# A cross-attention kernel with layer norm: a new hand-written order for its first twelve and last eight pairs of row tiles, one residual product taken from TensorE, the statistics of tile 62 computed on ScalarE, the last store in two halves

## The chip, the cores and the metric

The kernel runs on one core of one Trainium2 chip. The metric is device microseconds (us) of that core, the median of several runs. Engines are named as in the profile: PE is TensorE's matrix products, PEld its weight loads, DVE is VectorE, ACT is ScalarE, POOL is GpSimd, SP is SyncE, which here only issues DMA transfers. Transfers can also be issued by ACT and POOL, and then take time on those engines' own instruction streams.

## What is computed

`x` has 4 batches of 2048 rows of 512 numbers, `ctx` has 4 batches of 77 rows; there are 16 heads of 32 columns. Everything is float32.

```python
q = x @ wq;  k = ctx @ wk;  v = ctx @ wv                   # then split into 16 heads of 32
s = q @ k.T / sqrt(32);  s = where(mask, -inf, s)          # 77 keys per row and head
out = softmax(s) @ v @ wo + x                              # residual
y = (out - mean(out)) / sqrt(var(out) + 1e-5) * gamma + beta
```

## The kernel before, in words

The 8192 rows are 64 tiles of 128 rows. Two tiles make a pair (numbers 0 to 31); four tiles make a group, for which the queries are computed together. A float32 matrix product with 512-wide weights is made of three products of rounded parts (high by high, high by low, low by high), so each projection of one tile's worth of output is 12 matrix instructions.

Nothing of the order is left to a scheduler. The string `ORDER` lists the whole program as some 2,100 words. A letter says what, a number says for which tile, pair or group part, and a part number follows a dot. The program emits the words in that order, so each engine executes its own words strictly in the order in which they stand; between engines only data and buffers make anything wait. The words that matter here, with the lines of the kernel before:

- On PE: `Qn` (line 290) a query product of 12 instructions; `Sn` (L414) the scores of tile n, 64 small instructions into four PSUM banks; `Vn` (L507) weights by values for pair n, 32 instructions into two banks, and `Wn` (L522) the same for one tile alone, used for tiles 62 and 63; `On` (L579) the output projection of tile n, 12 instructions; `Xn` (L566) adds the residual `x` into tile n's PSUM bank by a product with an identity matrix, ahead of `On`.
- On DVE: `Tn.j` (L431) masks four heads' scores and takes their row maxima (4 instructions, each followed by the reading of an accumulator); `qn` (L304) copies queries out of PSUM; `rn` (L456) reciprocals of the softmax sums; `tn` (L482) transposes a tile's weights in 32x32 blocks; `bn.i` (L540) and `dn` make the low part of the attention output; `+n` (L588) adds the residual and frees the bank; `$n` (L591) adds it in place in PSUM; `sn` (L630, L632) mean and variance of a tile; `yn` (L649) subtracts the mean and multiplies by gamma, in place; `zn` (L652) scales by the inverse deviation and adds beta.
- On ACT: `en.j` (L446) four heads' exponentials with their sums; `an.i` and `cn` (L536) the high part of the attention output; `in` (L269) casts of `x`; `kn` (L617) and `%n` (L645) scale and shift a tile by its statistics.
- On POOL: `nn` (L461) multiplies the exponentials by the reciprocals, `mn.i` (L473) half of that; `jn` (L273) low parts of `x`; `fn` (L621, L622) multiplies by gamma and adds beta; `un` (L636, L637) and `@n` (also L641) the inverse deviation of a tile.
- Transfers: `Pn.c` with a last letter s, a or g (L493, issued by SP, ACT or POOL): one of 12 copies that move pair n's transposed weights into the layout that `Vn` reads; `Un.c` the same for one tile, ahead of `Wn`; `xn` loads rows, `gn` loads transposed rows, `wn` (L625) stores a finished tile.

So a tile goes through PE scores, DVE maxima, ACT exponentials, DVE reciprocals, POOL normalisation, DVE transposition, 12 transfers, PE weights-by-values, ACT and DVE splitting, PE output projection, residual, statistics and the final pass. A tile's final pass has two forms: `@`, `%`, `f` put it on ACT and POOL, and `u`, `y`, `z` put it on DVE. The string `SLOTS` gives every buffer of every pool by hand: its row "mm" says which of the 8 PSUM banks each product takes, so a product can only start when the bank's last reader, some word on DVE or ACT, is done. The string `PADS` gives for each `Q` and `O` a number of empty instructions on PE's sequencer between its 12 matrix instructions.

From about pair 6 to pair 22 the order repeats every two tiles. Before that stand the weight preparation, keys and values; after it there are no more queries to load and the tiles drain.

Of the kernel before, what the change touches and what calls it, by code (L numbers as in the profile page):

```python
# [33 lines left out]
for b in range(4):  # L34
# [17 lines left out]
e1.3 F2 T2.2 j5 t0 e1.1 Q6 i4 F1 g7 r1 Y1 e2.0 F3 L1 T3.2 n1 Q5 x1 T3.1 e2.1 Y0 q6 R2 T3.3 e3.3 j4 t1 B0 e2.3 P0.6s  # L52
x3 e3.1 B2 D0 i7 q7 Z0.s T3.0 P0.10s e3.0 q5 P0.2s S4 P0.7s D2 e3.2 Z3.s S6 T4.0 P0.4s e2.2 G1 B1 g6 G2 Z1.s G0
Z2.s T4.3 e4.3 P0.3s r3 G3 P0.0s Q9 n3 T4.1 P0.1s T4.2 e4.2 P0.9s D1 P0.8s r2 n2 e4.0 t3 P0.5s Q8 P0.11s e4.1 T6.0
T6.3 i6 t2 Q10 e6.0 r4 P1.0s T6.2 n4 P1.8s T6.1 e6.1 S5 P1.2s q10 x2 q8 Q11 e6.2 j6 P1.11s T5.3 P1.1s T5.2 e5.3
P1.10s T5.1 P1.9s t4 j7 e6.3 P1.4s S7 P1.6s Q14 T7.0 P1.7s e7.0 q9 P1.3s r6 T7.3 P1.5s n6 e7.3 T7.2 x0 q11 Q13 g8
e7.2 T5.0 Z13.s T7.1 g9 e7.1 Z6.s M16.4 Z10.s S9 q13 Z11.s e5.0 q14 V0 r7 t6 n7 e5.1 V1 a0.1 T9.1 e5.2 t7 Q15 a1.0
b0.1 a1.1 P3.4s r5 T9.2 Z12.s n5 e9.2 b1.0 P3.1s b1.1 P3.8s O2 e9.1 T9.3 P3.2s t5 P3.0s a0.0 P3.5s i8 T9.0 P2.2s S8
e9.0 +2 j8 P3.3s T8.3 O3 P2.6s e9.3 b0.0 P3.6s T8.1 P3.10s T8.2 i9 P2.8s r9 s2 P3.11s S10 e8.2 j9 P3.9s +3 O1 P3.7s
T8.0 e8.0 P2.9s q15 s3 P2.3s n9 e8.1 P2.7s T10.0 P2.4s O0 T10.1 e8.3 x7 T10.2 v1 P2.1s +1 g11 e10.0 T10.3 P2.11s  # L60
Q12 +0 Z9.s k3 r8 Z4.s s1 n8 e10.3 P2.5s t9 Z5.s k2 g10 S11 s0 e10.1 f3 P2.0s V3 t8 e10.2 Q19 T11.1 P4.3s f2 a3.1
q12 P2.10s a3.0 e11.1 T11.3 w3 b3.0 x5 T11.0 Z8.s i11 v0 q19 P4.0s e11.0 b3.1 O7 x6 r10 P4.6s T11.2 n10 k1 P4.2s
S12 P4.4s k0 +7 P4.10s S13 e11.3 T12.1 f1 w2 s7 Q16 P4.9s e11.2 T12.3 P4.5s T12.2 P4.1s e12.2 T12.0 f0 P4.8s t10 x4
# [747 lines left out]
```

## Time and profile before

| what | us |
|---|---|
| median of 3 runs | 512.98 (512.11 to 513.15) |
| the profiled execution | 511.94 |
| its span, first to last instruction | 510.1 |
| PE busy | 499.4 |
| DVE busy | 470.7 |
| ACT busy | 463.2 |
| POOL busy | 421.6 |

The span is the time from the first to the last record of the profiled execution; the 1.8 us between it and the time of the same execution lie outside the records. Busy time is the time in which an engine has at least one instruction in work. "Waits" tell for each engine what released it after an idle time. A "timeline" lists single instructions with start and duration; matrix instructions overlap, so the time that one takes from the next is the distance of two starts, not the duration shown.

### The profile page before, as it was taken

Reading aid. Unit: us, or ns where it says so; the run is one execution under the profiler, and the core shown is the slowest. Engines: PE = TensorE matmul, PEld = TensorE weight load, DVE = VectorE, ACT = ScalarE, POOL = GpSimd, SP = SyncE. Lnnn points to the kernel's source line nnn. Section 1 sums busy time; section 2 is a strip of 40 time slices with the busy share of each in tenths; the row PEclk is TensorE's granted clock in tenths of the full one; section 3 lists DMA queues with packets and bytes.
Section 4 is the critical chain, followed back from the end, with each engine's and each line's share of the span. In section 5 each row is a group of like instructions: output and inputs, shape, how many; then the busy total and the mean of one; then the engine's idle time right before and its main releaser. Section 6 shows DMA issues by size and latency. Waiting matters only on the chain.

```text
span 510.1 us, 21817 instructions
## 1 busy us (share of the span) xinstructions
PE 499.4 (98%) x6835; PEld 384.7 (75%) x6835; DVE 470.7 (92%) x2565; ACT 463.2 (91%) x2221; POOL 421.6 (83%) x389
## 2 busy tenths in 40 slices
PE   8999999999999999999999999999999999999994
PEld 6987777777777777777777877777777767776673
DVE  5798999999999999999999999999999899999897
ACT  5699999998999999999999999999999999899620
POOL 2573756999978898989889898888899689999896
PEclk9999999999999999999999999999999999999999
DMA  8947767867977687687778678685787895688655
GB/s 304 399 137 216 191 171 173 251 190 239 267 222 219 189 238 209 200 243 207 229 206 245 200 217 238 187 243 161 218 223 210 225 224 168 174 242 259 176 174 214
DMA packets 58995, 110.95 MB, mean 217 GB/s; under 512 B 9398, under 2 KB 11790, under 8 KB 58886
## 3 DMA queue, kind: packets, MB, share of 16 engines
q1 hardware_dynamic: 55094, 102.22, 68.5%
q0 software_dynamic: 2512, 5.84, 4.1%
q10 hardware_dynamic: 1280, 1.51, 1.1%
q8 instruction: 60, 0.98, 0.9%
q14 instruction: 49, 0.40, 0.3%
HBM read 41.79 MB, written 16.78 MB: 115 GB/s over the span
## 4 chain that ended last, share of the span: by engine, by line
PE 79%; POOL 6%; DVE 5%; DMA 4%; ACT 2%; issue 1%; SPq 1%; DVEq 0%; POOLq 0%
PE pq L290 32%; PE po L579 25%; PE sc L414 10%; PE pa L507 9%; DMA PT<-B 3%; ACT pbuf L446 2%; DVE B L482 2%; PE pv L341 2%; POOL PT L493 1%; PE pk L313 1%; DMA stage_a<-wk 1%; DVE pbuf L431 1%; POOL o L621 1%; POOL mvt L637 1%; POOL o L622 1%
## 5 line engine op out<-in xcount | busy, mean ns | idle before, releaser
L446 ACT ACTIVATE pbuf<-pbuf,nm 128x77 f32<-128x77 f32 x1024 | 352.5, 351 | 4.2 <-DVE nm L431 4.0
L446 ACT ACTIVATION_READ_ACCUMULATOR pbuf<-pbuf,nm 128x1 f32 x1024 | 196.2, 192 | 0.0
L431 DVE CUSTOM_DVE_ANT_0 pbuf<-sc,mb 128x77 f32<-128x77 f32 x1024 | 171.3, 233 | 8.0 <-PE sc L414 4.3
L461 POOL TENSOR_TENSOR pbuf<-pbuf,ri 128x1232 f32<-128x1232 f32 x63 | 142.8, 2267 | 30.4 <-DVE ri L456 26.2
L579 PE MATMUL po<-woh,AH 128*128 128x512 f32 x256 | 102.2, 399 | 1.8 <-DVE nm L431 1.4
L290 PE MATMUL pq<-xth,wqh 128*128 128x512 f32 (+1 forms) x256 | 101.3, 396 | 0.3
L579 PE MATMUL po<-woh,AL 128*128 128x512 f32 x256 | 100.0, 391 | 0.2
L579 PE MATMUL po<-wol,AH 128*128 128x512 f32 x256 | 99.8, 390 | 0.0
L482 DVE STREAM_TRANSPOSE B<-pbuf 128x1280 f32<-128x1280 f32 x64 | 95.9, 1500 | 2.9 <-POOL pbuf L473 1.4
L290 PE MATMUL pq<-xtl,wqh 128*128 128x512 f32 (+1 forms) x256 | 98.1, 383 | 0.0
L290 PE MATMUL pq<-xth,wql 128*128 128x512 f32 (+1 forms) x256 | 98.1, 383 | 0.0
L431 DVE DVE_READ_ACCUMULATOR2_ANT nm<- 128x1 f32 x1024 | 84.7, 83 | 0.0
L273 POOL TENSOR_TENSOR xtl<-xtf,xth 128x1024 fp32r<-128x1024 f32 x28 | 67.2, 2406 | 5.8 <-ACT xth L269 5.8
L622 POOL TENSOR_TENSOR o<-o,bet 128x512 f32<-128x512 f32 x52 | 67.2, 1293 | 4.1
L414 PEld LDWEIGHTS sc<-kct,q 32*64 32x64 f32 x4096 | 51.3, 130 | 22.8 <-issue 10.8
L621 POOL TENSOR_TENSOR o<-o,gam 128x512 f32<-128x512 f32 x52 | 68.3, 1314 | 0.2 <-issue 0.2
L414 PE MATMUL sc<-kct,q 32*64 32x77 f32 x4096 | 60.7, 238 | 0.0
L507 PE MATMUL pa<-PT,vsb 96*32 96x256 f32 x992 | 59.7, 382 | 0.0
L579 PEld LDWEIGHTS po<-woh,AH 128*128 128x128 f32 x256 | 48.0, 188 | 14.8 <-PE pa L507 1.0
L290 PEld LDWEIGHTS pq<-xth,wqh 128*128 128x128 f32 x256 | 48.0, 188 | 12.4 <-issue 1.2
L579 PEld LDWEIGHTS po<-woh,AL 128*128 128x128 f32 x256 | 48.0, 188 | 11.5 <-DVE AL L540 1.4
L579 PEld LDWEIGHTS po<-wol,AH 128*128 128x128 f32 x256 | 48.1, 188 | 9.9 <-issue 0.5
(120 smaller groups left out, 640.0 us busy)
## 6 DMA issues: line engine op xcount, KB each, us to landing
PT<-B SPq DMA_DIRECT2D x339, 128.0 KB
xtf<-xT SPq DMA_DIRECT2D x28, 512.0 KB
o<-x SPq DMA_DIRECT2D x56, 256.0 KB
out<-o SPq DMA_DIRECT2D x56, 256.0 KB
PT<-B POOLq DMA_DIRECT2D x26, 128.0 KB, 4.2
stage_a<-wk SPq DMA_DIRECT2D x4, 256.0 KB
stage_b<-wo SPq DMA_DIRECT2D x4, 256.0 KB
stage_a<-xT SPq DMA_DIRECT2D x2, 512.0 KB
```

Source lines behind the costliest of these rows:

```text
L273: nc.gpsimd.tensor_tensor(l[:, c : c + 2], fx.pop((g, c)), xh[g][:, c : c + 2].bitcast(F32), ALU.subtract)
L290: nc.tensor.matmul(pq, w[:, c, m * P : (m + 1) * P], r[g][:, c, rs], start=(n == 0), stop=(n == 11))
L341: nc.tensor.matmul(pv[: rows.stop - rows.start], ctx_s[c][i][:, rows], v[c], start=(n == 0), stop=(n == 11))
L414: mm = nc.tensor.matmul(sc[j][r0 : r0 + SR, g * NK : (g + 1) * NK], qs[q, g, rs.start + r0 : rs.start + r0 + SR], kct[q, g, t // TPB, keys ...
L431: nc.vector.tensor_tensor_reduce(pb[:, h // 2, (h % 2) * NK : (h % 2 + 1) * NK], scs[t][j][:, g * NK : (g + 1) * NK], mb[:, t % TPB, keys_ ...
L446: nc.scalar.activation(pb[:, h // 2, (h % 2) * NK : (h % 2 + 1) * NK], pb[:, h // 2, (h % 2) * NK : (h % 2 + 1) * NK], AF.Exp, bias=nmax[t ...
L461: nc.gpsimd.tensor_tensor(pv, pv, rv.to_broadcast((P, NP, 2, NK)), ALU.mult)
L482: nc.vector.transpose(bt.rearrange("p c q r -> p q c r"), pbuf[t % NPB].rearrange("p q (c r) -> p q c r", c=5),)
L507: nc.tensor.matmul(pas[b, g // 2][HD * j : HD * (j + 1), (g % 2) * BLK : (g % 2 + 1) * BLK], vsb[:, 2 * b // TPB, h % 2, HD * (h // 2) : H ...
L579: nc.tensor.matmul(pos[t], a[:, c, rs], w[:, c, :], start=(first and c == 0 and n == 0), stop=(c == NC_D - 1 and n == 2),)
L621: nc.gpsimd.tensor_tensor(o, o, gam, ALU.mult)
L622: nc.gpsimd.tensor_tensor(o, o, bet, ALU.add)
```

## The change

The order of the words is new in two stretches. From pair 0 to about pair 9 and from tile 52 to the end the same words stand in another order, and "mm", the other buffer rows and `PADS` follow. Between them the order of the words on PE, DVE and ACT is as before, except for a few loads of `x` that stand a few words earlier or later. The empty instructions of `PADS` are 1,719 in place of 1,468.

These words differ:

- `X49` is gone; tile 49's residual is added by `$49` on DVE.
- Tile 48's final pass is `u48`, `y48`, `z48` in place of `@48`, `%48`, `f48`.
- `$52` and `$58` become `+52` and `+58`.
- `s62` becomes `=62`, new: two passes of ACT over tile 62's PSUM bank, the first a copy scaled by -1/512 whose accumulator gives minus the mean, the second a square of value minus mean whose accumulator gives 512 times the variance. `u62` and `y62` take those instead.
- `z63` and `w63` become `>63.0 <63.0 >63.1 <63.1`, new: the final pass and the store of tile 63 in halves of 256 columns, the first half stored by SP, the second by ACT.
- Of the transfers, `P25.4`, `P27.0` and `P29.6` go from SP to POOL, `P26.9` from ACT to SP, `U62.8` from SP to ACT, `U63.3` from POOL to ACT.

The order of the words on PE in the last stretch, before and after:

```text
before: S52 V23 S53 Q59 Q58 Q57 S54 Q56 V24 S55 O46 X49 O49 S56 O47 S57 V25 O48 Q61 Q63 S58 Q62 V26 S59 Q60 O50
        S60 O53 X51 S61 O51 V27 S62 O52 V28 O55 S63 O57 O56 X63 V29 X62 O54 O58 V30 O59 O61 O60 W62 W63 O62 O63
after:  S52 V23 S53 Q58 Q56 Q57 S54 Q59 S55 O46 V24 S56 O47 O49 V25 S57 O48 Q61 S58 Q62 Q63 Q60 S59 V26 O50
        S60 X51 O53 S61 O51 S62 V27 O52 V28 O55 O54 S63 X62 O57 X63 V29 O56 O58 V30 O59 O61 O60 W62 W63 O62 O63
```

The ends of `ORDER`, and the code:

```diff
-a30.0 U62.9s U63.10g s58 U62.11a U62.7s U63.7g O59 %53 $57 U62.1s U63.6g a30.1 U63.3g s57 U62.6s U62.10a @58 w52
-b30.0 U63.1a U63.2s b30.1 u57 O61 U63.8a y57 f53 U63.5a s54 U62.0a z57 %58 y54 w57 U63.9a O60 $59 f55 +61 s61 s59
-W62 @61 $60 w55 w53 s60 W63 u54 c62 w50 %61 u59 d62 O62 c63 u60 y59 z59 f61 d63 w59 z54 w56 y60 O63 z60 f58 w61 s62
-w49 w54 y62 w60 s63 u62 w58 y63 u63 z62 z63 w62 w63
+s57 m63.0 P30.7a %55 b29.1 O58 u57 t62 %53 f55 %52 t63 U62.10a U62.2s V30 U62.4a U62.1s U62.8a +58 U63.0s f53 a30.0
+s58 U63.4s O59 U62.0a $56 a30.1 U63.11s b30.0 U62.3a U62.9s s54 U62.11a U62.7s U63.7g U63.1a y57 U63.6g U62.6s
+U63.9a s56 U62.5g U63.8a U63.10g b30.1 O61 U63.2s u56 $59 U63.5a w55 z57 U63.3a @58 O60 y56 w46 f52 %58 +61 s61 s59
+W62 @61 y59 W63 $60 c62 u59 y54 f58 c63 d62 O62 %61 z59 s60 w59 w57 d63 u60 w53 y60 O63 w52 u54 =62 z60 w58 f61 y62
+w60 z54 z56 w54 s63 u62 w61 y63 w56 u63 z62 w62 >63.0 <63.0 >63.1 <63.1
...
+    def stats_act(t):
+        mv = mvs[t, 1] = tiny.tile([P, 4], F32, tag="mvt", bufs=64 - LATE, name=f"mvt_{t}")
+        nc.scalar.activation(od[t], pos[t], AF.Copy, scale=-1.0 / D, accum_out=mv[:, 3:4])
+        nc.scalar.activation(od[t], pos[t], AF.Square, bias=mv[:, 3:4], accum_out=mv[:, 1:2])
+        by_act.add(t)
+
     def rsqrt_one(t):
         mv = mvs[t, 1]
-        nc.gpsimd.tensor_tensor(mv[:, 2:3], mv[:, 1:2], eps[:, :1], ALU.add)
+        if t in by_act:
+            nc.gpsimd.tensor_scalar(mv[:, 2:3], mv[:, 1:2], 1.0 / D, EPS, ALU.mult, ALU.add)
+        else:
+            nc.gpsimd.tensor_tensor(mv[:, 2:3], mv[:, 1:2], eps[:, :1], ALU.add)
         nc.gpsimd.tensor_tensor(mv[:, 2:3], mv[:, 2:3], mhalf[:, :1], ALU.pow)
...
     def centre(t):
         o = pos.get(t, od[t])
-        nc.vector.scalar_tensor_tensor(o, o, mvs[t, 1][:, 0:1], gam, ALU.subtract, ALU.mult)
+        m, op = (3, ALU.add) if t in by_act else (0, ALU.subtract)
+        nc.vector.scalar_tensor_tensor(o, o, mvs[t, 1][:, m : m + 1], gam, op, ALU.mult)
...
+    def finish_half(t, i):
+        cols = slice(i * D // 2, (i + 1) * D // 2)
+        nc.vector.scalar_tensor_tensor(
+            od[t][:, cols], pos[t][:, cols], mvs[t, 1][:, 2:3], bet[:, cols], ALU.mult, ALU.add
+        )
+
+    def store_half(t, i):
+        cols = slice(i * D // 2, (i + 1) * D // 2)
+        (nc.sync, nc.scalar)[i].dma_start(out[t * P : (t + 1) * P, cols], od[t][:, cols])
```

More of the change, by code (lines that the diff above doesn't have):

```diff
@@ new lines @@
+b26.1 e59.1 z48 x53 X51 f42 T60.1 w49 O53 P28.8s T60.0 k47 T60.3 e59.3 T60.2 t58 P28.4g e60.0 S61 P28.10g x55
+P28.2g e60.2 r59 P28.3s O51 T61.3 P28.6g n59 P28.1s +53 e60.1 P28.5s T61.0 w48 T61.2 x56 T61.1 e60.3 S62 f47 P28.0s
+t59 V27 e61.1 r60 T62.1 a27.0 T62.0 n60 P29.9s O52 a27.1 s51 e61.3 P29.11s T62.3 x52 b27.0 w42 e61.2 s53 P29.1g x60
+V28 P29.0g P29.8s $50 k46 P29.7g P29.2s T62.2 P29.6g e61.0 b27.1 P29.4g x54 O55 t60 P29.3g P29.10s a28.0 u51 x59
+a28.1 @53 e62.3 r61 +52 n61 b28.1 O54 e62.1 b28.0 y51 +55 P29.5a f46 t61 e62.2 S63 z51 e62.0 X62 T63.2 w51 O57
```

129 lines of the change are left out of this document (62 added, 67 removed).

## The prediction

> **What bounds the kernel now.** I read the busy time by stretches first, then the chain of waits in order of time, then the waits of the last stretch, then single instructions.
>
> ```profile
> 68.00:85.00 17.00, 17.00 (x303) 12.71 (x303) 16.59 (x82) 16.47 (x81) 9.53 (x5) 1.00 0.61 158
> ...
> 289.00:306.00 17.00, 17.00 (x220) 13.32 (x219) 16.38 (x83) 16.66 (x82) 15.48 (x14) 1.00 0.71 208
> ```
>
> The columns are the stretch, its length and the busy time (with instructions) of PE, PEld, DVE, ACT, POOL, then the granted clock. PE is busy in all of 17.00 us, early and in the middle. DVE, at 16.38, and ACT, at 16.66, have 0.6 and 0.3 us to spare. So what PE is spared in these stretches comes off the end, and what the others are spared does not.
>
> ```profile
> 440.00:460.00 20.00, 20.00 (x372) 14.20 (x370) 19.79 (x127) 20.00 (x109) 18.79 (x18) 1.00 0.71 201
> 460.00:478.00 18.00, 17.14 (x183) 11.96 (x180) 17.86 (x87) 18.00 (x100) 16.15 (x24) 1.00 0.89 248
> 478.00:495.30 17.30, 16.91 (x94) 12.21 (x94) 15.67 (x30) 5.27 (x10) 15.81 (x22) 1.00 0.55 157
> ```
>
> Here it is different. From 440 to 478 PE, DVE (19.79 of 20.00, 17.86 of 18.00) and ACT are all full, and PE already stands still for 0.86 us in the second row. After 478 the exponentials are over and ACT has room.
>
> ```profile
> PE po L579 <- DVE nm L431: 1.4, 2, 0.9
> ...
> DVE B L482 <- POOL pbuf L473: 1.4, 1, 1.4
> ...
> DVE pbuf L431 <- PE sc L414: 0.8, 1, 0.8
> DVE B L482 <- POOL pbuf L461: 0.8, 2, 0.5
> ...
> DVE o L588 <- PE po L579: 0.7, 1, 0.7
> ...
> DVE po L591 <- PE po L579: 0.4, 1, 0.4
> PE po L579 <- DVE xth L652: 0.4, 1, 0.4
> ```
>
> These are the waits from 395 us, where the two orders part, to 510 us: sum, times, longest. DVE stands idle for 1.4 + 0.8 + 0.8 + 0.7 + 0.4 = 4.1 us in all, and PE's products wait for DVE for 1.4 + 0.4 us. So PE and DVE hold each other up in turn. The last 115 us are bound by these two together, and the question of this change is how much of DVE's 4.1 us of idleness the new order fills.
>
> **The change part by part.**
>
> *PE's own work.* The price of a product, and of a change of kind, from the chain of waits (start, length, what):
>
> ```profile
> 109.40 0.88 PE sc L414 x55
> 110.28 5.68 PE po L579 x24
> 115.96 2.72 PE pq L290 x12
> 118.68 0.88 PE sc L414 x55
> ...
> 148.42 5.66 PE pq L290 x24
> 154.08 5.44 PE po L579 x24
> 159.52 0.88 PE sc L414 x53
> 160.40 1.86 PE pa L507 x32
> ...
> 468.10 2.89 DVE B L482 x2
> ```
>
> A product that follows a product takes 2.72 us. A run of three takes 118.68 - 110.28 = 8.40, a run of four 159.52 - 148.42 = 11.10: 0.24 and 0.22 more than three and four times 2.72. So each run of products costs some 0.22 once, whatever its length. Counting the words, before `S20` the runs fall from 17 to 15, between there and `S52` they stay 16, and behind `S52` they fall from 16 to 15. The early part is worth -0.44 us, the late one -0.22. The empty instructions cost nothing that I can see: `PADS` gives the stretch at 110 0 to 8 per product and the one at 148 12 to 22, and the runs cost the same in both. More than 22 does not occur in the new `PADS`.
>
> ```profile
> 416.90 1.02 PE L566 MATMUL po<-o,ident 128*128 128x512 f32 x2
> 417.36 0.80 PE L579 MATMUL po<-woh,AH 128*128 128x512 f32 x1
> ...
> 420.96 0.95 PE L414 MATMUL sc<-kct,q 32*64 32x77 f32 x64
> ```
>
> `X49` with `O49` takes 420.96 - 416.90 = 4.06, which is 1.34 over a product. About 0.3 of it is a wait inside for the low part of pair 24, so the residual product itself is worth 1.0. Behind `S52` PE thus has 1.2 us less to do (1.6 if the wait goes too).
>
> *DVE's own work.* Starts of its instructions in a full stretch, and of maxima:
>
> ```profile
> 397.46 0.23 DVE L431 CUSTOM_DVE_ANT_0 pbuf<-sc,mb 128x77 f32<-128x77 f32 x1
> 397.61 0.23 DVE L431 CUSTOM_DVE_ANT_0 pbuf<-sc,mb 128x77 f32<-128x77 f32 x1
> ...
> 485.34 0.69 DVE L591 TENSOR_TENSOR po<-po,xth 128x512 f32<-128x512 f32 x1
> 485.94 0.74 DVE L652 SCALAR_TENSOR_TENSOR xth<-po,mvt,bet 128x512 f32<-128x512 f32 x1
> 486.59 0.69 DVE L630 BATCH_NORM_STATS2 st<-po 128x6 f32<-128x512 f32 x1
> ...
> 487.42 0.67 DVE L591 TENSOR_TENSOR po<-po,xth 128x512 f32<-128x512 f32 x1
> ```
>
> By starts, `$` costs 0.60, `z` 0.65 and `s` 0.83 (`y`, of the same kind as `z`, 0.65); a maximum costs 0.15. The change adds `$49`, `y48`, `z48` and removes `s62`: 0.60 + 0.65 + 0.65 - 0.83 = +1.1. `z63` in halves is two instructions, an estimate of +0.2. DVE has 1.3 us more to do. ACT loses `%48` and one transfer issue, POOL loses `f48`; ahead of the last exponentials neither is what PE waits for, so I give nothing for them.
>
> *DVE's idleness.* Adding up each engine's own words from `S52` on, waits left out, shows who is late. Ahead of `O61` PE has 12 `S` (0.88), 8 `V` (1.86), 4 `X` (1.0), 22 products and 15 runs: 92.6 us. Up to the low part of pair 30, which `O61` needs, DVE has 48 `T` (0.65), 14 transpositions (1.44), 13 `s`, 12 residuals, 8 `y` and `z`, 16 `b` and 8 `q` (0.60, as `$`), 14 reciprocals and two mask rows (0.3): 92.1. So DVE could be there first, and idles. In the new order PE has 91.4 and DVE, with `$49`, one `s` and one `y` more, 94.2: DVE has little reason to idle any more, and PE waits for it. For pair 24 and `O49` the same count gives 21.5 on DVE against 22.7 on PE before, and 26.3 against 25.3 after. Of DVE's 4.1 us the 0.7 of L588 stands ahead of the change (`+44`). The other 3.4 can go to nothing or stay; I leave 1.0, since scores and maxima still meet within 0.1 us at several tiles. DVE's idleness goes from 4.1 to 1.7.
>
> *The end.*
>
> ```profile
> 500.31 0.40 PE L579 MATMUL po<-woh,AL 128*128 128x512 f32 x1
> ```
> ```profile
> L645 ACT ACTIVATE o<-po,mvt 128x512 f32<-128x512 f32 x2 | 1.6, 782 | 1.1 <-DVE mvt L632 1.1
> ```
> ```profile
> L446 ACT ACTIVATION_READ_ACCUMULATOR pbuf<-pbuf,nm 128x1 f32 x1024 | 196.2, 192 | 0.0
> ```
> ```profile
> 505.48 1.40 DVE L652 SCALAR_TENSOR_TENSOR xtl<-po,mvt,bet 128x512 f32<-128x512 f32 x2
> ...
> 506.25 0.99 SPq L625 DMA_DIRECT2D out<-xtl  x2
> ```
>
> `O62` ends at 500.71. The new statistics are two passes of ACT, by the nearest rows 0.78 + 0.19 + 0.78, some 1.85 us with the hand-overs; `y62` overwrites what the second pass reads, so it waits for both, and behind it on DVE are queued `z54`, `z56`, then `s63`, `y63`, `z62` and the two halves, for which the last stores wait. DVE has `z59`, `s60`, `d63`, `y60`, `z60` ahead of `y62`, so it meets the wait late: between 0 and 1.0 us, I take 0.6. The last pass ends at 506.88 and the span at 510.1, 3.2 us for the last stores.
>
> ```profile
> GB/s 22 171 402 410 395 402 149 0 52 380 417 380 417 402 395 432 387 410 350 424 320 0 0 0 0 60 432 395 350 402 268 0 0 0 0 0 0 0 0 0
> ```
>
> In this row (slices of 0.275 us from 500 us) they run at some 400 GB/s, so a store of 256 KB lasts 0.65 us and half of it 0.33; the last one ends earlier by 0.3 to 0.65, I take 0.4. The Trainium skill, "DMA: Bandwidth & Descriptors", section "Issuing engines are not separate DMA queues", says that issuing from several engines saves only the issuing time. By it the half on ACT's queue would be worth at most half of the 0.99 that two issues take on SP; no run here shows it, and 0.5 in place of 0.4 would make the sum -1.4.
>
> *The sum:* -0.44 (early runs) + 1.3 (DVE's work) - 2.4 (its idleness) + 0.6 (`y62`) - 0.4 (store) = -1.3 us. The profiled execution took 511.94, so it would be 510.6; the median of the runs shown is 512.98, 1.0 higher, and takes the same step to **511.6**. Ends: with 0.7 of idleness left, no wait at `y62` and the full store, -0.44 + 1.3 - 3.4 - 0.65 = -3.2, 509.8; with all idleness kept, 1.0 at `y62` and nothing for the store, -0.44 + 1.3 + 1.0 = +1.9, 514.9.
>
> **The rivals.**
>
> *DVE's idleness stays.* PE now waits for DVE, so the scores come later, and DVE waits for them: the two go on in turn. For it: the closeness of the two sums. Against it: DVE's total is now the longer one. -0.44 + 1.3 + 0.6 - 0.4 = +1.1: 514.1.
>
> *PE is the bound after all.* Then its 0.44 + 1.2 (or 1.6) come off `O62`, and from there on the tail is 1.85 + 3 x 0.65 + 0.83 + 2 x 0.65 + 0.9 = 6.8 us to the last pass, where it was 506.88 - 500.71 = 6.2; with the store -0.44 - 1.4 + 0.6 - 0.4 = -1.6: 511.4.
>
> *The last pair's transfers come too late* (slower). `t62` and `t63` now follow each other, behind pair 29's low part, so all 24 `U` transfers start together, 11 in place of 9 of them on ACT, and eight of these stand behind `a30.0`, which waits for `V30`.
>
> ```profile
> L493 ACTq DMA_DIRECT2D PT<-B x11: 592/593/1345, 478.1 to 491.7; - x11
> ...
> DMA to landing us min/median/max: 2.3/3.4/3.5
> ```
> ```profile
> 484.41 1.93 PE L507 MATMUL pa<-PT,vsb 96*32 96x256 f32 x32
> ...
> 495.34 1.95 PE L522 MATMUL pa<-PT,vsb 96*32 96x128 f32 x64
> ```
>
> An issue takes 0.59 us on ACT and lands 3.4 later. From the end of `V30`, 486.3 before, two `a` and eight issues are 5.9 us, the last landing 495.0 or so, against 496.3 for `W63`. It decides from the point at which `V30` ends more than some 1.3 us later against `W63` than now; with 3 us it costs 1.7, and with DVE's idleness kept half the way the sum is -1.3 + 1.7 + 1.7 = +2.1: 515.1.
>
> *The early order stalls PE,* which waits for nothing there now. The same sums of own work give DVE no worse a place against PE than before, so this is small: one wait of 2 us, 513.6.
>
> **How the numbers follow.** Chances: forecast 0.55, PE as the bound 0.15, idleness stays 0.15, late transfers 0.10, early stall 0.05. About 0.2% (1.0 us) is what a measurement of this kernel can tell from no change. The forecast's own spread reaches from 510.2 to 512.9, so two thirds of it and most of the PE case are faster by more: 0.37 + 0.14 = 0.51. Half of the idleness case and the transfers are slower by more: 0.07 + 0.10 + 0.01 = 0.18. 0.31 is left for within. The range, 509.8 to 514.3, leaves out the late transfers and some of the ends.
>
> **What would show it.** Right: DVE's waits behind 395 us fall from 4.1 to below 2.5 us while PE's products wait longer for DVE than 1.8; `S20` starts 0.4 us earlier; `y62` waits for ACT; the span behind the last pass shrinks below 3.2. Wrong: DVE waits as long as before (first rival), PE's sums of waits do not rise (second), `W62` or `W63` is released by a transfer (third), or PE has a gap before 130 us (fourth).

## The result and the profile after

| | median, us | runs | lowest to highest | profiled execution | its span |
|---|---|---|---|---|---|
| before | 512.37 | 21 | 511.34 to 514.25 | 511.94 | 510.1 |
| after | 515.07 | 21 | 512.47 to 518.45 | 513.25 | 511.5 |

The kernel is slower: the ratio is 1.0048, with a 95% interval of 1.0038 to 1.0058. (One disturbed run of 520.52 us is left out of the highest.) Two things have to be explained: the 1.4 us between the two profiled spans, and the 1.8 us by which the usual run of the kernel after lies above its own profiled execution; the kernel before lies 0.4 above its own.

The busy time by stretches of the kernel after; the columns are those of the prediction, with the DMA engines' mean busy share and GB/s last:

```profile
60.00:70.00 10.00, 9.79 (x121) 6.57 (x120) 8.54 (x43) 9.13 (x53) 6.90 (x5) 1.00 0.73 196
...
110.00:120.00 10.00, 8.69 (x180) 6.24 (x179) 7.44 (x54) 8.89 (x47) 8.20 (x9) 1.00 0.98 272
...
289.00:306.00 17.00, 17.00 (x220) 13.32 (x219) 16.42 (x89) 16.66 (x84) 15.52 (x13) 1.00 0.72 216
440.00:460.00 20.00, 20.00 (x349) 14.84 (x347) 19.80 (x132) 20.00 (x109) 18.85 (x24) 1.00 0.65 174
460.00:478.00 18.00, 17.60 (x188) 12.39 (x180) 17.73 (x86) 17.20 (x92) 17.13 (x21) 1.00 0.98 269
```

And the same stretch of the kernel before:

```profile
110.00:120.00 10.00, 10.00 (x140) 7.94 (x128) 9.62 (x53) 8.85 (x49) 8.81 (x8) 1.00 0.67 192
```

From 110 to 120 us PE, which never stood still there, loses 1.3 of 10 us, DVE is less busy too (7.44 in place of 9.62 us), and the DMA engines are full (0.98 in place of 0.67). In the steady part nothing has changed (289 to 306 us). From 460 to 478 PE's gap has shrunk from 0.86 to 0.40 us; there, too, the DMA engines are now full. Single instructions of PE in the timeline of the kernel after, with what ended the wait ahead of each in brackets:

```profile
65.24 0.62 PE L507 MATMUL pa<-PT,vsb 96*32 96x256 f32 x2
66.07 3.66 PE L507 MATMUL pa<-PT,vsb 96*32 96x256 f32 x62 [0.21 <-DMA vsb<-v]
...
113.84 0.94 PE L414 MATMUL sc<-kct,q 32*64 32x77 f32 x64 [0.95 <-DMA o<-x]
...
116.58 0.80 PE L414 MATMUL sc<-kct,q 32*64 32x77 f32 x6
117.60 0.90 PE L414 MATMUL sc<-kct,q 32*64 32x77 f32 x58 [0.23 <-DVE nm L431]
...
161.78 0.94 PE L414 MATMUL sc<-kct,q 32*64 32x77 f32 x63
...
397.88 0.95 PE L414 MATMUL sc<-kct,q 32*64 32x77 f32 x64
```

and `S20` and `S52` of the kernel before:

```profile
159.45 0.95 PE L414 MATMUL sc<-kct,q 32*64 32x77 f32 x64
...
395.45 0.95 PE L414 MATMUL sc<-kct,q 32*64 32x77 f32 x64
```

`S20` starts 2.33 us later, where the forecast had 0.44 earlier, and `S52` still 2.43 later. The sites are `V0` with `V1` (0.8 us: 4.41 from the start of `V0` to the next product, in place of 3.60), `S14` (1.0) and `S15` (1.0, between its first six instructions and the others). Behind `S52` the new order does gain: `O62` starts 100.23 us after it, in place of 101.77. The waits from 395 us on:

```profile
DVE ri L456 <- ACT pbuf L446: 1.1, 1, 1.1
DVE o L588 <- PE po L579: 0.7, 1, 0.7
PE sc L414 <- DVE q L304: 0.6, 1, 0.6
DVE xtl L662 <- POOL mvt L646: 0.6, 1, 0.6
PE pa L507 <- DVE mvt L632: 0.4, 1, 0.4
DVE pbuf L431 <- PE sc L414: 0.2, 1, 0.2
```

DVE's idleness is 1.1 + 0.7 + 0.6 + 0.2 = 2.6 us, where it was 4.1. The 0.6 of it at L662 lies behind `O62`. PE's wait of 0.4 at L507 carries DVE's name, but it is that of `V28`, which is for transfers, as shown below. The end, from ACT's statistics to the last stores (two timelines and the GB/s row, slices of 0.275 us from 500):

```profile
501.58 0.60 ACT L636 ACTIVATE xtl<-po 128x512 f32<-128x512 f32 x1 [2.03 <-PE po L579]
...
502.89 0.19 ACT L637 ACTIVATION_READ_ACCUMULATOR xtl<-po,mvt 128x1 f32 x1
```
```profile
502.22 0.75 DVE L662 SCALAR_TENSOR_TENSOR xtl<-po,mvt,bet 128x512 f32<-128x512 f32 x1 [0.57 <-POOL mvt L646]
503.12 0.76 DVE L659 SCALAR_TENSOR_TENSOR po<-po,mvt,gam 128x512 f32<-128x512 f32 x1
...
507.37 0.87 DVE L666 SCALAR_TENSOR_TENSOR xtl<-po,mvt,bet 128x256 f32<-128x256 f32 x2
...
508.27 0.38 ACTq L672 DMA_DIRECT2D out<-xtl  x1
```
```profile
GB/s 0 141 387 410 410 395 425 387 432 387 402 417 402 209 372 410 134 0 0 156 395 380 22 209 424 372 432 395 75 0 283 395 384 376 387 82 0 0 0 0
```

The last pass ends at 508.24, and the span at 511.5: 3.3 us for the stores, level with the 3.2 before. From the start of `O62` to the end of the span there are 13.39 us, where there were 12.88. DVE stands still for 0.57 us ahead of `z60`, which waits for `u60` on POOL; the kernel before has no wait of DVE behind `O62`.

### The profile page after: what moved, and what is told of

It reads as the page before. It is cut to its first block, busy times and chain, and to the rows that moved or that the text cites. A ratio compares the mean times of both kernels' runs of the same rounds, so it can differ in the third digit from the quotient of the medians.

```text
span 511.5 us, 22056 instructions
## 1 busy us (share of the span) xinstructions
PE 499.4 (98%) x6833; PEld 385.4 (75%) x6833; DVE 470.8 (92%) x2567; ACT 464.1 (91%) x2224; POOL 419.9 (82%) x388
## 4 chain that ended last, share of the span: by engine, by line
PE 66%; DVE 12%; DMA 7%; POOL 4%; ACT 4%; issue 3%; SPq 2%; ACTq 0%; DVEq 0%; POOLq 0%
PE pq L290 25%; PE po L579 24%; PE sc L414 8%; PE pa L507 8%; DVE pbuf L431 4%; ACT pbuf L446 3%; DMA vsb<-v 2%; DVE B L482 2%; POOL pbuf L461 2%; DMA stage_a<-xT 2%; DVE st L630 1%; DMA stage_a<-wk 1%; DMA PT<-B 1%; PE pv L341 1%; POOL xtl L273 1%
## 5 line engine op out<-in xcount | busy, mean ns | idle before, releaser
L414 PEld LDWEIGHTS sc<-kct,q 32*64 32x64 f32 x4096 | 52.0, 130 | 25.0 <-issue 11.9
L622 POOL TENSOR_TENSOR o<-o,bet 128x512 f32<-128x512 f32 x51 | 66.0, 1293 | 4.0
L414 PE MATMUL sc<-kct,q 32*64 32x77 f32 x4096 | 61.8, 238 | 2.2 <-DMA o<-x 0.9
L507 PE MATMUL pa<-PT,vsb 96*32 96x256 f32 x992 | 60.4, 382 | 0.6 <-DVE mvt L632 0.4
```

Of the source, the lines that this page charges most:

```text
L414: mm = nc.tensor.matmul(sc[j][r0 : r0 + SR, g * NK : (g + 1) * NK], qs[q, g, rs.start + r0 : rs.start + r0 + SR], kct[q, g, t // TPB, keys ...
L507: nc.tensor.matmul(pas[b, g // 2][HD * j : HD * (j + 1), (g % 2) * BLK : (g % 2 + 1) * BLK], vsb[:, 2 * b // TPB, h % 2, HD * (h // 2) : H ...
L622: nc.gpsimd.tensor_tensor(o, o, bet, ALU.add)
```

## The experiments

The first theory was that the early order costs the time, through transfers that stand late on SyncE's (SP's) queue. Two rivals: the last stretch and its tail cost it; or ACT's casts of xT do, whose loads the change also puts one place later throughout the steady part, which the section on the change does not say (group 14's load stands 25 words ahead of its cast, not 89). In the kernels of this section, except e11, line numbers are 11 lower than in the kernel after (its L414 is L403). "Against before" is the difference to the median of the kernel before on the same chip.

This table goes by the distance between PE's instructions in each profiled execution, since `S0` itself starts between 20.96 and 22.26 us: from `S0` to `S20`, `S20` to `S52`, `V27` to `V28`, and from `O62` to the end of the span.

| kernel | median | against before | S0-S20 | S20-S52 | V27-V28 | O62-end |
|---|---|---|---|---|---|---|
| before | 512.37 | | 138.25 | 236.00 | 6.57 | 12.88 |
| after | 515.07 | +2.70 | 140.46 | 236.10 | 5.33 | 13.39 |
| e1 | 511.84 | -0.65 | 138.44 | 235.96 | 5.64 | 13.47 |
| e2 | 514.61 | +2.12 | 140.49 | 237.80 | 6.57 | 13.03 |
| e3 | 514.19 | +1.70 | 140.70 | 235.86 | 5.99 | 13.34 |
| e4 | 514.41 | +1.92 | 140.80 | 235.94 | 7.22 | 13.37 |
| e5 | 514.98 | +2.52 | 140.32 | 236.12 | 6.73 | 13.38 |
| e6 | 513.77 | +1.31 | 139.92 | 236.04 | 5.20 | 13.37 |
| e7 | 514.08 | +1.62 | 138.42 | 236.26 | 6.89 | 13.36 |
| e8 | 512.70 | +0.24 | 138.10 | 235.85 | 5.71 | 13.34 |
| e9 | 512.91 | +0.53 | 139.39 | 236.12 | 4.96 | 13.54 |
| e10 | 511.24 | -1.14 | 138.06 | 235.88 | 4.89 | 13.62 |
| e11 | 516.75 (one run) | | 140.99 | 236.03 | 6.92 | 13.41 |
| e12 | 512.99 | +0.61 | 138.56 | 235.95 | 6.35 | 13.92 |
| e13 | 514.40 | +1.77 | 141.11 | 237.91 | 4.95 | 13.66 |
| e14 | 512.85 | +0.22 | 139.45 | 235.97 | 4.90 | 13.52 |
| e15 | 511.27 | -0.85 | 137.97 | 236.06 | 4.89 | 13.90 |
| e16 | 514.89 | +2.77 | 139.71 | 236.13 | 6.37 | 13.81 |

### e1 and e2: one stretch old, one new

```diff
-ORDER, SLOTS and PADS up to S52: after
+ORDER, SLOTS and PADS up to S52: before
```

> The order, buffers and empty instructions of the kernel before up to the scores S52 (all that is issued up to 395 us), and from there those of the kernel after, with tile 62's statistics on ScalarE and the halved last pass. First theory: the early order costs the time (S20 starts 2.33 us later after the change than before it, S52 2.43 us later) and the last stretch gains about 1 us (the offset falls from 2.43 us at S52 to 1.36 us at the end of the last pass); so this kernel stands 0.7 to 1.3 us below the kernel before, near 511.4 us. Rival: the last stretch and its tail cost the time, and the offset of the early stretch is taken up anyway by work that waits later; so it stands as far above the kernel before as the kernel after does, near 515.1 us.

```diff
-ORDER, SLOTS and PADS from S52 on: after
+ORDER, SLOTS and PADS from S52 on: before
```

> The converse: the kernel after up to S52, and from there the kernel before, with tile 62's statistics on VectorE and a whole last pass. First theory: the whole offset of 2.4 us stays, and the last stretch gives nothing back; 514.8 to 516.5 us, at or above the kernel after. Rival that the last stretch costs the time: equal to the kernel before within 0.5 us, 512.4 us.

e1: 511.84 us, ratio to before 0.9991 (0.9976 to 1.0006). e2: 514.61, ratio 1.0053 (1.0034 to 1.0071). So the loss lies ahead of `S52`, and the rival that the last stretch costs the time falls. In the profiled executions the last stretch gives something back (from `S52` to `O62` e1 needs 99.59 us, the kernel before 101.77); e1's median alone does not show it. One thing does not fit yet: e2's profiled execution lost 1.8 us more between `S20` and `S52`, where its order is that of before but for xT and a few loads of x.

### e3 and e4: two transfers moved forward

```diff
-Q8 i7 t3 x11 n2
+Q8 i7 t3 x4 n2
...
-T13.1 a2.1 x4 T12.1
+T13.1 a2.1 x11 T12.1
```

> The kernel after with two words of its order exchanged: tile 4's x is loaded where tile 11's x was (49 us, into the free buffer 7) and tile 11's where tile 4's was (108 us, into buffer 4, behind the store of tile 3). Nothing else is moved. First theory, its part on the buffer: tile 4's x, issued at 108.37 us and landed near 113 us, is what VectorE waits for 2.37 us at 113.30 and PE then at S14 and S15 (0.95 + about 1 us); with it gone S20 starts about 2 us earlier (near 159.8 us) and the time falls by 1.5 to 2.5 us, to 512.6 to 513.6 us. Rival that the last stretch costs the time: S20 may start earlier, but the time stays within 0.5 us of the kernel after, 515.1 us. A third: another wait (the store of tile 3 itself, which waits for GpSimd's f3) comes instead, and less than 0.7 us is gained.

```diff
-T6.3 Z13.s t2 e6.0 Z0.s e6.3
+T6.3 Z0.s Z1.s Z2.s t2 e6.0 e6.3
...
-e5.3 Z1.s j6
+e5.3 j6
...
-T7.3 Z2.s q9
+T7.3 Z13.s q9
```

> The kernel after with the two small transfers of batch 0's last 19 keys (issued at 60.72 and 62.73 us) put directly behind that of its first 58 keys (near 53 us), and the transfer of batch 3 that stood ahead of these put to the later place. First theory: V0 and V1 take 3.6 us again in place of 4.41, since the values are there when the first product asks for them, and PE is 0.8 us earlier from 67 us on; the time falls by 0.8 us (514.3 us) if nothing later takes this up, and by nothing if tile 4's x, which lands near 113 us whatever PE does, sets the time of S14 by itself. Rival that the last stretch costs the time: no change, 515.1 us.

e3: 514.19 us, `S20` at 161.89. e4: 514.41, `S20` at 162.67. Neither brought `S20` forward. In e3 DVE now waits at its next residual, for tile 5's x, as e6 shows below (first fence); in e4 `V0` runs through, and `V1` waits (second fence):

```profile
115.64 0.69 DVE L577 TENSOR_TENSOR o<-po,o 128x512 f32<-128x512 f32 x1 [2.21 <-PE sc L403]
```
```profile
65.75 1.93 PE L496 MATMUL pa<-PT,vsb 96*32 96x256 f32 x32
68.93 1.93 PE L496 MATMUL pa<-PT,vsb 96*32 96x256 f32 x32 [1.24 <-DMA vsb<-v]
```

The waits were named rightly as transfers, but each one taken away uncovers the next on the same queue. In the brackets the one named is only the transfer that came last; e4 had just moved the `Z` transfers forward, so `V1`'s 1.24 us are put down to pair 1's regrouping transfers, the last of which now stand behind `Z13` on SP (with `Z13` behind them, in e14, `V1` does not wait).

### e5, e6 and e7: xT, and tiles 4 and 5 together

```diff
-s9 e15.3 r14 n14
+s9 e15.3 g12 r14 n14
...
-e16.3 g12 T17.3
+e16.3 g13 T17.3
...
-b6.1 g13 n17
+b6.1 g14 n17
```

> The kernel after with the loads of xT of groups 12 to 26 each put at the place of the load before it, as the kernel before has them (group 14's load then stands 84 words ahead of its cast in the order, not 25). Nothing else is changed. Second theory, formed on the first four runs: ScalarE's cast waits 2.9 us for these loads in the kernel after's profiled execution (before: 0.4) and 6.5 us in the profiled execution of the kernel after with the late stretch of before, where PE loses 1.8 us between S20 and S48; so the just-in-time loads cost the usual run about 1.5 us and make the runs scatter. Expected: 513.3 us median (1.8 below the kernel after), lowest and highest closer together, ScalarE's waits for xT below 0.6 us, and still 2.3 us late at S20. First theory alone (all is lost before S20): no change, 515.1 us.

```diff
-t3 x11 n2
+t3 x4 n2
...
-a2.1 x4 T12.1
+a2.1 x5 T12.1
...
-P5.0s x5 e12.1
+P5.0s x13 e12.1
...
-e13.0 x13 f0
+e13.0 x11 f0
```

> The kernel after with four loads of x exchanged round: tile 4's at the place of tile 11's (buffer 7, 49 us), tile 5's at the place of tile 4's (buffer 4), tile 13's at the place of tile 5's (buffer 5), tile 11's at the place of tile 13's (buffer 2). First theory, mended: exchanging tile 4 alone took S14's wait from 1.09 to 0.47 us but left S15's at 1.06, because tile 5's x, issued at 110.34 us, is then what VectorE waits for (2.21 us ahead of 115.64); with both early, S14 and S15 together lose under 0.4 us in place of 2.1, S20 starts near 160.0 us, and the median falls by 1.3 to 2 us against the kernel after, to 513.1 to 513.8 us. Rival: the place is set by VectorE's own work or by the transposes there, S15 still waits, and the time is that of the kernel after.

e7 is both edits.

> Both of the other two at once: the loads of x of tiles 4 and 5 early, and the loads of xT of groups 12 to 26 one place earlier. Both theories: the gains add, 3 to 3.5 us below the kernel after, near 511.8 us, and level with the kernel that has the early order of before and the late stretch of after (511.84 us). If the two waits are one and the same lateness seen twice, the gain is that of the larger alone, 513.3 us.

e5: 514.98 us, no change that the median shows, though ACT no longer waits for xT at all (2.9 us in the kernel after, from 130 to 395 us). e6: 513.77, and `S15`'s wait is gone, but `S14` still loses 1.03 us. e7: 514.08. In its profiled execution the early stretch was as short as that of before (138.42 us from `S0` to `S20`). Part of that is luck: e9, below, has the same early order, and its profiled execution waits at `V1`, `S13` and `S14` and needs 139.39. And yet e7 was no faster than e6. In its profile PE stood still in another place:

```profile
464.89 1.93 PE L496 MATMUL pa<-PT,vsb 96*32 96x256 f32 x32 [1.94 <-DVE nm L420]
```

This is `V28`. `nm` feeds nothing of it, so the name in the bracket is only the last event of that moment. Its two banks, last read by DVE for `T62.0` and `T62.3`, were free by 462 us. What is left are its 12 regrouping transfers.

### e9 and e10: room for pair 28's transfers

Pair 28's transposed weights take the buffer of pair 26, so none of the 12 transfers can start before `V26`. The new order has `V26` at 445.84 us and `V28` at 465.36 (19.5 us); before, it was 440.35 and 463.82 (23.5 us). Among those transfers on SP's queue stood a store and two loads of 256 KB that nothing needed yet. e9 moves them in e7, e10 in e1:

```diff
-S61 P28.10g x55 P28.2g
+S61 P28.10g P28.2g
...
-T61.0 w48 T61.2 x56 T61.1 e60.3 S62 f47 P28.0s t59
+T61.0 T61.2 T61.1 e60.3 S62 f47 P28.0s w48 x55 x56 t59
```

> The kernel with both early mendings (loads of x of tiles 4 and 5 early, loads of xT one place earlier), and in the late stretch the store of tile 48 and the loads of x of tiles 55 and 56 (256 KB each), which stood on SyncE's queue among the regrouping transfers of pair 28, moved behind the last of these. Third theory: V26 stands 5.5 us later in the new late order, so pair 28's twelve transfers have 19.1 us in place of 23.5 between V26, which frees their buffer, and V28; the DMA engines are 80 to 99 % busy in that time, and V28 waits as long as the run's transfers happen to be late (0.37 us in the profiled execution after, 1.94 in that of the kernel with both early mendings). With 0.75 MB out of their way (3.3 us at the 230 GB/s of that stretch) V28 waits under 0.4 us, its distance from V27 falls from 6.9 to 5.4 us, and the median falls by 1 to 1.5 us, to 512.6 to 513.1 us. Rival: what spreads the runs lies elsewhere; V28's wait goes, another takes its place (tile 55's or 56's x late), and the median stays within 0.4 us of 514.08.

> The same three transfers moved in the kernel with the early order of before and the late stretch of after (511.84 us; V28 waits 0.67 us in its profiled execution, and its runs spread from 510.4 to 514.8). Third theory: 510.9 to 511.3 us, and a narrower spread. Rival: no change within 0.4 us.

e9: 512.91 us, 1.2 below e7. e10: 511.24 us, ratio to before 0.9979 (0.9967 to 0.9990). In e10 `V28` follows the last product without a gap:

```profile
462.21 0.39 PE L568 MATMUL po<-woh,AL 128*128 128x512 f32 x1
462.53 1.29 PE L496 MATMUL pa<-PT,vsb 96*32 96x256 f32 x20
```

In all five kernels with this edit (e9, e10, e13, e14, e15) `V28` stands 4.89 to 4.96 us behind `V27`; in the eleven profiled executions of the new late order without it, 5.20 to 7.22, on average 6.2. That is shown, then: with these three words behind pair 28's transfers `V28` follows at once in every execution; where the three stand among them, the transfers land late, by a different time in each execution, and PE pays for it.

The edit does more than take 0.75 MB out of their way. The load of tile 55's x goes into the buffer of tile 49, so it waits until tile 49's store has landed, and while it waits the last four of pair 28's transfers on SP stand behind it. The kernel after, first SP's own wait from 452 to 463 us, then its timeline: the load, and the last of the twelve transfers, `P28.0`, as the first of three.

```profile
SPq L548 <- DMA out<-o: 2.1, 1, 2.1
```
```profile
456.65 0.33 SPq L548 DMA_DIRECT2D o<-x  x1
...
460.08 3.17 SPq L493 DMA_DIRECT2D PT<-B  x3
```

In the eleven executions this wait is 2.1 to 4.9 us, and `P28.0` is issued 0.05 to 1.8 us after `V27` has started. In the five `P28.0` stands ahead of the load and is issued 3.9 to 4.4 us before `V27`. The DMA engines are as busy in both. From 455 to 465 us, in the kernel after and in e13, which is the kernel after with this edit alone (the DMA share is the number before the last):

```profile
455.00:465.00 10.00, 9.96 (x186) 6.87 (x184) 9.76 (x65) 10.00 (x56) 9.91 (x10) 1.00 0.91 259
```
```profile
455.00:465.00 10.00, 9.88 (x187) 7.19 (x186) 9.69 (x75) 10.00 (x54) 9.83 (x10) 1.00 0.90 266
```

No run separates the wait on the queue from the 0.75 MB themselves.

### e11: the kernel after once more

> The kernel after, unchanged, profiled once more: its profiled execution of 513.25 us stands 1.8 us below its median. What a usual run of 514 to 516 us loses beside that one is to be seen: by the third theory V28 waits 1.5 us or more and S20 stands where it stood (161.8 us); by the second (xT just in time) S52 minus S20 is 1 us or more above 236.1 us; by the first S20 itself is later.

It fell on an execution of 516.75 us. `S20` is at 162.40 (0.6 later than in the first profile), and the rest is `V28`. First PE's timeline, then the stretches (the granted clock is the number ahead of the last two):

```profile
467.29 2.52 PE L507 MATMUL pa<-PT,vsb 96*32 96x256 f32 x32 [1.97 <-DVE nm L431]
...
470.33 0.63 PE L579 MATMUL po<-wol,AH 128*128 128x512 f32 x1
470.76 0.63 PE L579 MATMUL po<-woh,AL 128*128 128x512 f32 x1
...
472.22 0.39 PE L579 MATMUL po<-woh,AH 128*128 128x512 f32 x1
472.45 0.39 PE L579 MATMUL po<-wol,AH 128*128 128x512 f32 x1
```
```profile
467.00:470.00 3.00, 2.71 (x33) 1.50 (x34) 2.70 (x4) 1.65 (x8) 2.72 (x7) 0.75 0.90 328
470.00:473.00 3.00, 3.00 (x10) 2.40 (x11) 1.95 (x3) 3.00 (x17) 2.99 (x2) 0.68 1.06 263
```

After the wait of 1.97 us, which is 1.6 more than in the first profile, matrix instructions start 0.43 us apart, not 0.23, until 472: from `V28` to `O62` PE needs 34.30 us, where it needs 32.7 to 32.8 in every other kernel of the new late order. So the lower clock cost 1.5 us besides the wait.

### e8 and e12: the tail

```diff
->63.0 <63.0 >63.1 <63.1
+z63 w63
```

> The early order of before with the late stretch of after, and tile 63's last pass and store whole again instead of in halves. The prediction's term: the halves are worth 0.4 us, so 512.2 us. Rival, from the two profiled executions: VectorE's last passes take 0.87 us in halves against 0.74 whole, and from the end of the last pass to the end of the span there are 3.26 us with the halves and 3.22 without, so the halves bring nothing or cost 0.1 us: 511.7 to 511.9 us, and the time behind the last pass is 3.2 us again.

```diff
-u54 =62 z60 w58 f61 y62
+u54 z60 w58 f61 s62 y62
```

> The early order of before with the late stretch of after and a whole last pass (512.7 us; 13.34 us from O62's start to the end of the span), and tile 62's statistics on VectorE again, ahead of y62, in place of ScalarE. The prediction's two terms: VectorE does 0.87 us more, and y62 no longer waits 0.6 us for ScalarE, so 0.3 us slower (13.6 us from O62). Rival: y62's wait for ScalarE and the later order of the last passes cost more than VectorE's 0.87 us, as the kernel before has 12.88 us from O62 to the end: 0.2 us faster or more.

e8 (from e1): the median is 512.70, 0.9 above e1's, with intervals that overlap (0.9990 to 1.0022 against 0.9976 to 1.0006). Its profiled tail is 13.34 us against 13.47, and between the end of the last pass (505.58) and the end of the span are 3.3 us:

```profile
504.18 1.40 DVE L651 SCALAR_TENSOR_TENSOR xtl<-po,mvt,bet 128x512 f32<-128x512 f32 x2
504.95 0.99 SPq L614 DMA_DIRECT2D out<-xtl  x2
```

The traces show no gain from the halves; the medians would allow one, and this stays open. e12 (from e8): 512.99 us, and the tail 13.92 in place of 13.34. That tile 62's statistics on ScalarE are a gain is not shown: the two intervals overlap (0.9997 to 1.0030 against e8's 0.9990 to 1.0022), and executions that have them on ScalarE, too, show tails of 13.34 to 13.90 us.

### e13, e14, e15 and e16: the early order

e13 is the kernel after with the edit of e10 alone.

> The kernel after with the three transfers (tile 48's store, tiles 55's and 56's x) moved behind the last regrouping transfer of pair 28, and nothing else: the third theory's part undone alone. In the second profile of the kernel after (516.75 us) V28 waits 1.97 us, and the granted clock is 0.75 and 0.68 in the 5.7 us behind this wait, so that the twelve products there take 1.6 us more: a wait of 2 us costs 3.5. Third theory: V28 waits under 0.4 us in every run, no clock is lost, and the median falls by 1.2 to 1.8 us against the kernel after (515.07), to 513.3 to 513.9 us; what is left is the early stretch, 1 to 1.5 us above the kernel before. Rival: the wait is only moved, less than 0.5 us is gained.

514.40 us, 0.9 nearer to before than the kernel after; the intervals (1.0009 to 1.0045 and 1.0038 to 1.0058) overlap. `V28` no longer waits (4.95). But its profiled execution lost 1.8 us between `S20` and `S52`, as e2's had, and here it can be followed: ACT's cast waits for xT, then a low part on DVE waits for ACT, then PE for DVE.

```profile
253.31 1.05 ACT L258 CAST xth<-xtf 128x1024 fp32r<-128x1024 f32 x1 [2.49 <-DMA xtf<-xT]
```
```profile
260.88 1.29 DVE L529 TENSOR_TENSOR AL<-pa,AH 128x512 fp32r<-128x512 f32 x2 [0.92 <-ACT AH L525]
```
```profile
262.22 0.50 PE L568 MATMUL po<-woh,AL 128*128 128x512 f32 x1 [0.76 <-DVE AL L529]
```

Of the eight executions with xT one place later (after, e2, e3, e4, e6, e11, e13, e16) two (e2 and e13) lost 1.8 to 1.9 us between `S20` and `S52`; of the ten with xT as before, none did. From 130 to 395 us ACT's casts wait 6.5 us for xT in each of these two, 0.9 to 2.9 in the other six, and 0.4 in the kernel before. So the theory on xT, which e5's median did not bear out, holds for e13, where the chain is followed, and most likely for e2; two of eight do not tell how often it costs PE anything.

e14 is e9 with batch 0's values early, and `Z13` behind pair 1's transfers:

```diff
-e6.0 Z0.s e6.3
+e6.0 Z0.s Z1.s Z2.s e6.3
...
-T7.0 P1.2s e7.0
+T7.0 P1.2s Z13.s e7.0
```

> The kernel after with all that was mended: loads of x of tiles 4 and 5 early, loads of xT one place earlier, pair 28's transfers freed (together 512.91 us), and now the values of batch 0 early too, with the transfer for batch 3 that took their place put behind the last regrouping transfer of pair 1 (in the fourth run V0 no longer waited, but V1 did, 1.24 us, as pair 1's transfers stood behind the one for batch 3). The prediction's term for the early order (15 in place of 17 starts of products, 0.44 us less than the kernel before up to S20) should then show: S20 near 159.3 us, the median near 512.0 us. If PE still waits at V1, S13 or S14 by turns, the new early order has no slack for its transfers whatever single one is moved: S20 stays above 160 us and the median at 512.6 us or more, 1.4 us above the kernel with the early order of before (511.24 us).

512.85 us, `S20` at 160.41: the second of the two cases expected. `V0` and `V1` no longer wait, but `S13` and `S14` do:

```profile
101.14 0.94 PE L403 MATMUL sc<-kct,q 32*64 32x77 f32 x64 [0.50 <-DMA PT<-B]
...
113.35 0.87 PE L403 MATMUL sc<-kct,q 32*64 32x77 f32 x60 [0.97 <-DMA PT<-B]
```

This time the bracket is right. The kernel makes the scores that stand directly ahead of a pair's values' product wait for that pair's transfers (a dependence that it adds itself), so `S13` waits for pair 2's and `S14` for pair 4's. Pair 4's last transfers stood behind the loads of x and behind tile 3's store, which took 1.89 us of SP's queue (0.4 of it a wait for POOL; what held the rest the trace does not show); in the kernel after, with pair 4's last transfer as the first of the two at the end:

```profile
103.46 1.89 SPq L625 DMA_DIRECT2D out<-o  x1
...
108.37 0.53 SPq L548 DMA_DIRECT2D o<-x  x1
108.94 1.29 SPq L493 DMA_DIRECT2D PT<-B  x2
```

e15 puts them ahead, and pair 2's ahead of pair 4's, in e14; e16 does that in the kernel after:

```diff
-T11.3 P4.11s e11.3 T11.2 P2.4s j8
+T11.3 P2.4s e11.3 T11.2 P2.8s j8
...
-T12.3 x7 e12.2
+T12.3 P4.4s P4.2s P4.1s x7 e12.2
```

> The kernel with all that was mended (512.85 us; S20 at 160.41 us, with 0.54 us lost at S13 and 1.17 at S14), and now on SyncE's queue pair 2's regrouping transfers ahead of pair 4's (they are needed at S13, 10 us before pair 4's at S14), and pair 4's last three ahead of the load of tile 7's x and the store of tile 3, which blocks the queue. The scores ahead of a pair's values' product wait for that pair's transfers by the kernel's own rule, so S13 waits for pair 2's and S14 for pair 4's. Fourth theory, which puts the first and the third into one: what the change takes away everywhere is the time that a pair's twelve regrouping transfers have before its values' product (V0 3.6 us earlier, V4 4.8 us earlier, V28's buffer freed 5.5 us later). Expected: S13 and S14 no longer wait (under 0.3 us together in place of 1.7), S20 at 158.9 to 159.4 us, as the forecast had it, and a median of 511.2 to 511.7 us, level with the kernel with the early order of before (511.24 us). Rival, the early order without slack: another wait takes their place, 512.6 us or more.

> The kernel after with that one change alone (pair 2's regrouping transfers ahead of pair 4's, pair 4's last three ahead of tile 7's x and tile 3's store). Fourth theory: S13 and S14 wait under 0.3 us; tile 4's x, which moves 1 us later on the queue, may take part of it back at S15, and V0 still loses 0.7 us, so S20 is 0.8 to 1.2 us earlier than in the kernel after (161.78 us) and the median 513.9 to 514.3 us in place of 515.07. Rival: no change, 515.1 us.

e15: 511.27 us, ratio to before 0.9984 (0.9970 to 0.9998). e15 differs from the kernel after in nothing but the order of the words on SP's queue and the buffers of x that go with it, and the whole loss is gone. `S20` starts where the forecast had it:

```profile
159.10 0.95 PE L403 MATMUL sc<-kct,q 32*64 32x77 f32 x64
```

e16: 514.89, no gain in the median. In its profiled execution `S13` and `S14` do not wait any more, and from `S0` to `S20` it needs 139.71 us, 0.75 less than the kernel after; `V1` (1.0 us) and `S15` (1.0) still wait, as expected, and `V28` came late. What two mended places gain does not show in the median.

## Why the prediction was wrong, point by point

**The step that failed** is the fourth rival, "The early order stalls PE": "The same sums of own work give DVE no worse a place against PE than before, so this is small", with a chance of 0.05. The sums compared engines' work with each other. What the early order changed is the time that transfers have: `V0` starts 3.6 us earlier than before (65.24, not 68.81) and `V4` 4.8 us earlier (114.71, not 119.49), while the regrouping transfers, values and residual rows that they and their neighbours need stand on the same in-order queue among stores and loads. No single one was at fault. e3, e4 and e6 each removed a wait, and the next transfer on the queue took its place; with all of them in order (e15) the early stretch takes 137.97 us in place of 140.46. The sign that the prediction gave for this rival, a gap of PE before 130 us, is what the profile shows. Its price was one wait of 2 us; there were three places, and they cost 2.7 us against the forecast.

**The term of -0.44 us** for the early runs was not borne out in the kernel after, which needs 140.46 - 138.25 = 2.2 us more from `S0` to `S20`. As a sum of PE's own work it is not contradicted: e15 needs 138.25 - 137.97 = 0.28 less than before. But the five executions with the early order of before reach from 138.06 to 138.56, so the size of this gain is not shown.

**DVE's extra work and its idleness** (+1.3 - 2.4): the direction of the idleness was right, the mechanism was not. It fell from 4.1 to 2.6, not 1.7, and PE's waits for DVE did not rise above 1.8 but fell to 0.6 us. That is the sign of the second rival, PE as the bound. It had PE's own work behind `S52` shorter by 1.2 to 1.6 us, and from `S52` to `O62` the kernel after needs 1.5 us less than before (e15 2.1 us less).

**The end.** `y62` does start right behind the second of ACT's passes, which took 1.5 us together (501.58 to 503.08). But this held DVE up by some 0.24 us, not 0.6: `y62` starts 0.90 us after `z60`, where such an instruction takes 0.66. What the sum did not have is the 0.57 us that DVE waits for POOL ahead of `z60`. In the two executions with the last stretch of before the tail takes 12.88 and 13.03 us, in the others 13.34 to 13.92, also with the statistics on DVE (e12). No run takes the wait at `z60` away, so the cause of the longer tail stays open. The -0.4 of the half store is not in the traces.

**What no step had.** The third rival looked at the last pair's transfers only, and those were not late. Pair 28's were, in a buffer that became free 5.5 us later, behind a load that held SP's queue. And the loads of xT, one place later, were taken as nothing. Both cost little in the first profile of the kernel after, which is one of its fastest executions, and more in others. A rough account starts at the profiled execution of before, 511.94 us: +1.4 us in the profiled spans; +0.9 for `V28`, whose mean distance over eleven executions is 6.2 us, not 5.33; +0.14 for one loss of clock of 1.6 us in these eleven; +0.5 for the two late xT (1.8 and 1.9 us) in eight. That makes 514.9, and the median is 515.07. The means are of few executions of several kernels, and no median bears out the part of xT. The shift from a profiled execution to the median, 1.0 us in the prediction, is 0.4 for the kernel before over 21 runs and 1.8 for the kernel after.

The best versions are e10 (the early order of before) at 511.24 us, and e15 at 511.27. Both are faster than before, by 1.1 and 0.9 us; the new early order, mended, is worth nothing that these runs can tell.

## What to carry to other kernels

When the order on an in-order queue changes, write down for each product when its last transfer can start (its buffer free, its source written) and what stands ahead of it on the queue; a sum of engines' own work does not see this. A load or store that must wait for its buffer or its source holds up everything behind it. A transfer that lands just in time in the profiled execution can land late in others: `V28`, which lost 0.4 us in the first profile, lost 1.3 on the mean of eleven executions (6.2 us behind `V27`, and 4.9 when its transfers are early). And mend all such places before judging an order, since one at a time they hide each other.

## What the runs showed of the hardware

After a wait of PE of 1.97 us matrix instructions started 0.43 us apart, not 0.23 (e11). The granted clocks of 0.75 and 0.68 over two stretches of 3 us make 1.5 + 1.9 = 3.4 us at half the clock, an estimate. Waits of 1.94 (e7), 1.78 (e5) and 1.44 us (e4) at the same place were not followed by such a stretch. The Trainium skill, "TensorE: Matmul & The Clock Gate", section "Part 1: The HAM clock gate", says that TensorE falls to half its clock after an idle window of some 3.4 us, that it needs about as long a busy one to come back, and that the windows run freely. Half the rate and the length of the slow stretch agree. The idle time does not: here it was less than 2 us, and the measurement decides. This is one execution, and no run shows why this wait was followed by the lower clock and that of 1.94 us was not.

The landing of a transfer scatters between executions. SP's wait for tile 49's store to land was 2.1 to 4.9 us in eleven executions, and `V28`, which waited in all of them, started 4.5 to 6.7 us after the issue of its pair's last transfer. The DMA engines were 0.79 to 0.91 busy from 455 to 465 us. With the last transfer issued 4 to 6 us earlier against `V27` they were 0.86 to 0.90 busy, and `V28` did not wait in any of five. Whether the full engines make the scatter is not shown, since no run had them idle.

For the half store, the rule that the prediction named (the Trainium skill, "DMA: Bandwidth & Descriptors", "Issuing engines are not separate DMA queues") is what the traces agree with: 3.3 us from the last pass to the end with the halves on two queues (508.24 to 511.5), 3.2 with the whole store on one (506.88 to 510.1).
